# Half-width expert blocks behind the full ones in a two-layer AdaLN kernel with a mixture of experts

## The chip, the cores and the metric

The kernel runs on one core of a Trainium2 chip. The metric is the device time of one execution in microseconds. A profile shows the busy time of five engines: TensorE (PE, with its weight loads as PEld), VectorE (DVE), ScalarE (ACT), GpSimd (POOL) and the queue of SyncE (SP), which issues most DMAs.

## The reference, cut to what matters

Two AdaLN blocks over 8 sequences (b = 0 to 7) of 512 tokens and 128 channels, all float32:

```python
# layer 0
h = layernorm(x) * (1 + ca) + sa
x = x + ga * attention(h)                  # 16 heads of 8 channels, low-rank terms in q, k, v, o
h = layernorm(x) * (1 + cb) + sb
x = x + gb * moe(h)                        # 8 experts, 2 per token, 128 -> 512 -> 128, and a shared expert
# layer 1
h = layernorm(x) * (1 + ca) + sa
x = x + ga * selective_ssm(h)              # convolution, projection, scan along the sequence, projection
h = layernorm(x) * (1 + cb) + sb
x = x + gb * ffn(h)                        # pointwise convolution, 8 experts with gates (all computed), RMS norm, FFN
```

The part that is changed is `moe`: a router picks two of eight experts for each token, each expert is gelu(h W1 + b1) W2 + b2 with a hidden width of 512, the two results are weighted by the router's probabilities, and one shared expert is added for all tokens.

## The kernel before, in words

The program has three stretches. First comes the attention of layer 0, written as a row of "slots"; events that belong to the layer-0 experts (router, ranks, places, scatters) are hung on slots too. Then come "ticks": one pass of the loop at L1771 per block of expert work, with events of layer 0's routing of the last sequence and of layer 1's SSM hung on tick numbers by `when(t, ...)`. Last comes a tail of events without ticks, in which the experts of layer 1 are computed; it begins at tick number n, the number of blocks.

**Routing.** The eight sequences are in two parts, `PB = (6, 2)`: part 0 is b = 0 to 5, part 1 is b = 6 and 7. `place` gives each token a row within its expert's region of a DRAM tensor `x_rows[h]`, and `scatter` (L802) writes tokens there, with indirect DMAs on POOL. When all tokens of a part are placed, `table(h, step)` (L818) works out, on DVE and POOL, how many blocks of 256 rows (BLK) each expert has; the blocks of all experts stand in one row. There are `NBLK[h]` places for them: the number of full blocks that the tokens make, plus 7, because each of eight experts may leave its last block partly empty. That is 31 for part 0 and 15 for part 1. For each block the table holds the expert (`of`), the first row (`row0`) and the biases. `rows_back` (L881) works out where each token's two results will stand in `y_rows`.

**Ticks.** `work` (L1592) is the list of blocks: 31 routed blocks of part 0, 12 blocks of the shared expert for part 0, 15 routed blocks of part 1 and 4 of the shared expert, n = 62 in all. At tick i TensorE transposes the input of block i + 2 (`turn_in`, pxt), runs `up` of block i (L1056: ph, four matmuls of 256 columns, each followed by a gelu on ACT) and `down` of block i - 1 (L1064: pyb, eight matmuls of 128 columns, then a copy on ACT). A float32 matmul shows as two in the profile. For a routed block (`routed`, L949) the SP queue reads `of` and `row0` into registers and issues four DMAs: `xg` (the block's 256 rows, four ticks ahead), `w1b` and `w2b` (the expert's two weight matrices, 256 KB each, three and two ticks ahead, three buffers each) and `y_rows` (the result). A shared block (`everyone`, L1006) has its weights at hand and needs only `hl`, one load for two blocks.

**Behind the routed blocks of part 0.** From tick 32 on (`t0`, L1688) 48 indirect DMAs on POOL (`gather`, L1084) bring each token's two results back, and `combine` (L1098) adds them on DVE, weighted, to the shared expert's result. Then follow, per sequence, the statistics, the modulation and the convolution of the SSM (on DVE and ACT), the projection of four sequences at a time (`ssm_project`, pj), a chain of elementwise steps on ACT, DVE and POOL with a scan (`chain`, L1623), the projection out (`ssm_out`, py) and the lead-in to layer 1's FFN (`lead_in`, L1630): `ffn_pointwise` (L1383, pw), logits, ranks, gates. The gates of the first sequence go out at tick 61. The gathers and SSM of part 1 run in the tail beside layer 1's experts, whose products `t` are formed on DVE, and for odd experts of b = 0 to 3 on POOL (`expert_gate`, L1498).

**Order.** Each engine's instructions stand in the order in which the program pins them. DMAs on SP are placed in that queue by the scheduling layer.

Of the kernel before, what the change touches and what calls it, by code (L numbers as in the profile page):

```python
# [30 lines left out]

BLK = 256
# [3 lines left out]
NBLK = tuple(2 * n * S // BLK + NE - 1 for n in PB)  # L36
# [32 lines left out]
def tile_adaln_two_blocks(  # L69
# [144 lines left out]
    def folded(out, src):  # L214

        lead, n = list(src.shape[1:-1]), src.shape[-1]
        flat_n = math.prod(lead)
        names = "abc"[: len(lead)]
        sizes = dict(zip(names, lead))
        while n > 1:  # L220
            n //= 2
            if n > 1:
                dst = stat.tile([P, NC4 * NE * n], FP, tag=f"fold{n}", name=f"fold{n}", bufs=1)[:, 0 : flat_n * n]
                dst = dst.rearrange(f"p ({' '.join(names)} n) -> p {' '.join(names)} n", n=n, **sizes)
            else:
                dst = out.unsqueeze(len(lead) + 1)
            cut = (slice(None),) * (1 + len(lead))
            G.tensor_tensor(dst, src[cut + (slice(0, n),)], src[cut + (slice(n, 2 * n),)], ALU.add)
            src = dst
# [50 lines left out]
    y_rows = [dram.tile([NBLK[h] * BLK, D], FP, tag=f"y_rows{h}", name=f"y_rows{h}") for h in range(2)]  # L280
# [17 lines left out]
    with tc.tile_pool(name="at", bufs=2) as at, tc.tile_pool(name="sc", bufs=4, space=PSUM) as psc, tc.tile_pool(  # L298
# [371 lines left out]
        for h in range(2):  # L670

            def kept(shape, name, kind=FP):
# [10 lines left out]
                "shift": kept([P, NE], "shift"),  # L683
                "of": kept([P, NBLK[h]], "of", I32),
# [130 lines left out]
        TABLE = 3 + NF  # L815
        blocks = {}

        def table(h, step):  # L818

            hh, n, j = half[h], NBLK[h], CAP[h] // BLK  # L820
# [5 lines left out]
            if step == 0:  # L826
                own = stat.tile([P, NE], FP, tag="own", name="own")
                V.scalar_tensor_tensor(own, count[:, 0:NE], -float(CAP[h]), hh["next"], ALU.mult, ALU.add)
                cmp = tt(NE * j, "cmp").rearrange("p (e j) -> p e j", j=j)
                steps = stat.tile([P, CAP[0] // BLK], FP, tag="steps", name="steps")[:, 0:j]  # L830
                V.tensor_scalar(steps, count[:, 0:j], float(BLK), None, ALU.mult)
# [6 lines left out]
                ends = stat.tile([P, NE], FP, tag="ends", name="ends")  # L838
# [3 lines left out]
                ahead = stat.tile([P, NE], FP, tag="ahead", name="ahead")  # L842
                V.tensor_reduce(ahead, cmp, AX.X, ALU.add)
                V.tensor_tensor(ends, ends, ahead, ALU.add)

                V.tensor_scalar(ahead, ahead, float(BLK), None, ALU.mult)
                V.scalar_tensor_tensor(hh["shift"], count[:, 0:NE], -float(CAP[h]), ahead, ALU.mult, ALU.add)
                blocks["ends"] = ends
            elif step == 1:

                cmb = blocks["cmb"] = tt(n * NE, "cmb").rearrange("p (n e) -> p n e", e=NE)
                V.tensor_tensor(
                    cmb,
                    count[:, 0:n].unsqueeze(2).to_broadcast(shape),
                    blocks.pop("ends").unsqueeze(1).to_broadcast(shape),
                    ALU.is_ge,
                )
                of = tt(n, "of")
# [6 lines left out]
            elif step == 2:  # L865
                wide = tt(n * NE, "wide").rearrange("p (n e) -> p n e", e=NE)
                V.tensor_tensor(wide, blocks["cmb"], hh["shift"].unsqueeze(1).to_broadcast(shape), ALU.mult)
                row0 = tt(n, "of")
                V.tensor_reduce(row0, wide, AX.X, ALU.add)
                V.scalar_tensor_tensor(row0, count[:, 0:n], float(BLK), row0, ALU.mult, ALU.subtract)  # L870
                V.tensor_scalar(row0, row0, float(NE * CAP[h] - BLK), None, ALU.min)
                V.tensor_copy(hh["row0"], row0)
            else:

                f = step - 3
# [5 lines left out]
        def rows_back(h):  # L881
            hh = half[h]
            shape = [P, 2, PC[h], NE]
            tmp = fr.tile([P, 2 * PC[0] * NE], FP, tag="tmph", name="tmph", bufs=1)[:, 0 : 2 * PC[h] * NE]
            tmp = tmp.rearrange("p (k c e) -> p k c e", k=2, e=NE)
            V.tensor_tensor(
                tmp, hh["which"], hh["shift"].unsqueeze(1).unsqueeze(1).to_broadcast(shape), ALU.mult
            )
            yr = stat.tile([P, 2, PC[0]], FP, tag="yr", name="yr", bufs=1)[:, :, 0 : PC[h]]
            V.tensor_reduce(yr, tmp, AX.X, ALU.add)  # L890
# [20 lines left out]
        for i in range(TABLE):  # L911
            at_slot(32 * PB[0] + (45, 47, 49, 59, 60, 62, 63)[i], lambda i=i: table(0, i))
# [34 lines left out]
        shared, turned = {}, {}  # L947

        def routed(h, i):  # L949


            def locate(it):
                it["e"], it["r"] = (
                    nc.values_load(
                        half[h][name][0:1, i : i + 1],
                        engines=[mybir.EngineType.SP],
                        min_val=0,
                        max_val=most,
                        skip_runtime_bounds_check_because="held to the last one by a minimum",
                    )  # L960
                    for name, most in (("of", NE - 1), ("row0", NE * CAP[h] - BLK))
                )

            def fetch(it):
                if "r" not in it:
                    locate(it)
                it["xg"] = fr.tile([P, 2, D], FP, tag="xg", name="xg", bufs=4)
                Q.dma_start(out=it["xg"], in_=x_rows[h][bass.ds(it["r"], BLK), :].rearrange("(c p) d -> p c d", p=P))

            def fetch_1(it):  # L970
                it["w1"] = fr.tile([P, NF * P], FP, tag="w1b", name="w1b", bufs=3)
                Q.dma_start(out=it["w1"], in_=w1t[:, bass.ds(it["e"], 1), :].rearrange("p o f -> p (o f)"))

            def fetch_2(it):
                it["w2"] = fr.tile([P, NF, D], FP, tag="w2b", name="w2b", bufs=3)
                Q.dma_start(
                    out=it["w2"].rearrange("p f d -> p (f d)"),
                    in_=w2t[:, bass.ds(it["e"], 1), :, :].rearrange("p o f d -> p (o f d)"),
                )

            def turn_in(it):
                ps = bank("pxt")
                for c in range(2):
                    pin(T.transpose(ps[:, c, :], it["xg"][:, c, :], ident))  # L984
                it["x"] = fw.tile([P, BLK], FP, tag="xt", name="xt", bufs=3)
                V.tensor_copy(it["x"], flat(ps)[:, 0:BLK])

            def leave(it, py):
                yb = fw.tile([P, 2, D], FP, tag="yb", name="yb", bufs=3)
                A.copy(yb, py[:, 0:2, :])  # L990
                Q.dma_start(
                    out=y_rows[h][BLK * i : BLK * (i + 1), :].rearrange("(c p) d -> p c d", p=P), in_=yb
                )
# [5 lines left out]
                "fetch_2": fetch_2,  # L999
                "turn_in": turn_in,  # L1000
                "first": lambda py: None,
                "leave": leave,
                "bias": lambda f: half[h]["bias"][:, i, f : f + 1],
            }

        def everyone(b, i):  # L1006
# [4 lines left out]
            def fetch(it):  # L1011
# [3 lines left out]
                it["w1"], it["w2"] = ws1, ws2  # L1015
                it["x"] = turned[b][:, BLK * i : BLK * (i + 1)]

            def turn_in(it):
# [4 lines left out]
                it["gt"] = fw.tile([NE + 1, BLK], FP, tag="gt", name="gt", bufs=4)  # L1023
# [15 lines left out]
            def leave(it, py):  # L1039
# [7 lines left out]
                "fetch_2": lambda it: None,  # L1047
                "turn_in": turn_in,
                "leave": leave,
                "bias": lambda f: col("bs1", f),  # L1050
# [5 lines left out]
        def up(it):  # L1056
            ph = pair("ph").rearrange("p a (b t) -> p (a b) t", t=BLK)
            for f in range(NF):
                pin(T.matmul(ph[:, f, :], lhsT=it["w1"][:, f * P : (f + 1) * P], rhs=it["x"], start=True, stop=True))  # L1059
            it["hid"] = fw.tile([P, NF, BLK], FP, tag="hid", name="hid")  # L1060
            for f in range(NF):
                A.activation(it["hid"][:, f, :], ph[:, f, :], AF.Gelu_apprx_tanh, bias=it["bias"](f))

        def down(it):  # L1064
            py = bank("pyb")
            it["first"](py)
            for c in range(2):
                for f in range(NF):
                    pin(
                        T.matmul(  # L1070
                            py[:, c, :],
                            lhsT=it["hid"][:, f, c * P : (c + 1) * P],
                            rhs=it["w2"][:, f, :],
# [790 lines left out]
```

## Time and profile before

| | us |
|---|---|
| median of 6 runs | 1022.19 |
| lowest, highest | 1019.26, 1025.82 |
| the profiled execution | 1020.34 |
| its span, first to last instruction | 1018.5 |

| stretch of the profiled execution | us from the span's start |
|---|---|
| 31 routed ticks of part 0 | 541.8 to 663.8 |
| 12 shared ticks | 663.8 to 720.2 |
| 15 routed ticks of part 1 | 720.2 to 803.5 |
| 4 shared ticks, to the last ph | 803.5 to 830.5 |
| tail | 830.5 to 1018.5 |

The granted clock of TensorE is 0.99 over the span. A row of a group of instructions in the profile reads: line, engine, operation, what it writes <- what it reads, number; busy time and mean duration; idle time of the engine before it and what ended that. Helpers record under one line (L65 for DVE, ACT, POOL and SP), so these are told apart by the names of their tiles.

### The profile page before, as it was taken

What the parts mean: (1) busy time and instruction counts of PE and PEld (TensorE: products, weight loads), DVE (VectorE), ACT (ScalarE), POOL (GpSimd) and SP (SyncE); (2) the same over time, 40 slices, a digit from 0 to 9 for tenths busy, and PEclk for the clock granted to TensorE, in tenths of its full rate; (3) what the DMA queues carried; (4) which work ended last, traced back from release to release, by engine and by line L of the source; (5) the groups of instructions that cost most, each with busy time, mean ns of one, the idle gap of its engine ahead of it and who ended that gap; (6) DMA issues with size and microseconds to landing.
All of it is one profiled execution on the core that took longest, in us unless ns stands there. A gap on an engine that the chain in (4) does not pass through costs nothing.

```text
span 1018.5 us, 24175 instructions
## 1 busy us (share of the span) xinstructions
PE 983.6 (97%) x9540; PEld 649.3 (64%) x9540; DVE 659.1 (65%) x1310; ACT 608.1 (60%) x1335; POOL 479.6 (47%) x755
## 2 busy tenths in 40 slices
PE   9999999999999999999998999999999999898897
PEld 7455455555555545555558999988778666566565
DVE  6777787787877868687723112314787559777863
ACT  1365566666666666666674565545477465585654
POOL 3312133373553736445455213337735257564773
PEclk9999999999999999999999999999999999999899
DMA  6099500000000000000024778652464125223061
GB/s 177 1 287 284 176 3 12 1 12 23 7 28 2 27 8 10 25 2 31 9 80 135 227 241 253 195 147 65 125 167 134 31 66 170 83 81 129 21 214 36
DMA packets 94914, 94.89 MB, mean 93 GB/s; under 512 B 7848, under 2 KB 72832, under 8 KB 94800
## 3 DMA queue, kind: packets, MB, share of 16 engines
q1 hardware_dynamic: 90528, 84.65, 27.4%
q0 software_dynamic: 4096, 8.40, 2.7%
q8 instruction: 75, 1.23, 0.5%
q14 instruction: 39, 0.32, 0.1%
q10 hardware_dynamic: 176, 0.30, 0.1%
HBM read 61.96 MB, written 31.36 MB: 92 GB/s over the span
## 4 chain that ended last, share of the span: by engine, by line
PE 70%; DVE 12%; POOL 9%; ACT 3%; issue 3%; DMA 2%; POOLq 0%; DVEq 0%; SPq 0%; ACTq 0%
PE ps L542 22%; PE av L563 11%; PE pyb L1070 7%; PE ph L1059 7%; PE pm L493 5%; POOL yg L1090 4%; PE pe L1487 2%; PE r L1475 2%; DVE xc L65 2%; PE pqk L451 2%; DVE mpad L65 1%; DVE sh L65 1%; PE pmt L528 1%; PE pw L1387 1%; DVE t L65 1%
## 5 line engine op out<-in xcount | busy, mean ns | idle before, releaser
L65 ACT ACTIVATE es<-ps 128x512 f32<-128x512 f32 x512 | 273.5, 600 | 168.5 <-PE pm L493 125.5
L65 DVE TENSOR_REDUCE mpad<-pm 128x2 f32<-128x1024 f32 (+1 forms) x262 | 308.7, 1194 | 99.0 <-PE pm L493 91.5
L542 PE MATMUL ps<-qt,kt 32*128 32x512 f32 x1024 | 292.4, 629 | 0.5 <-DVE x L65 0.5
L493 PE MATMUL pm<-kt,qt 32*128 32x512 f32 x976 | 260.5, 632 | 0.7 <-DVE mpad L65 0.7
L563 PEld LDWEIGHTS av<-es,vaug 128*32 128x32 f32 x4096 | 104.2, 109 | 94.3 <-ACT es L65 35.9
L542 PEld LDWEIGHTS ps<-qt,kt 32*128 32x128 f32 x1024 | 99.7, 183 | 71.8 <-issue 29.7
L563 PE MATMUL av<-es,vaug 128*32 128x128 f32 x4096 | 137.7, 276 | 0.1
L65 ACT ACTIVATE hid<-ph,bias 128x256 f32<-128x256 f32 x184 | 72.0, 475 | 52.5 <-PE ph L1059 52.3
L807 POOL DMA_INDIRECT x_rows<-tok,ux x64 | 65.4, 1022 | 69.9 <-DMA x_rows<-tok,ux 63.7
L1070 PEld LDWEIGHTS pyb<-w2b,hid 128*128 128x128 f32 x736 | 90.1, 192 | 6.6 <-ACT hid L65 3.8
L1070 PE MATMUL pyb<-w2b,hid 128*128 128x128 f32 x736 | 91.7, 278 | 2.5 <-ACT hid L65 2.5
L1059 PE MATMUL ph<-xt,w1b 128*128 128x256 f32 x368 | 87.9, 382 | 0.0
L493 PEld LDWEIGHTS pm<-kt,qt 32*128 32x128 f32 x976 | 75.3, 183 | 16.6 <-DVE mpad L65 8.2
L1090 POOL DMA_INDIRECT yg<-y_rows,yrows x64 | 64.9, 1014 | 39.1 <-DMA hl<-h_chan 20.7
L65 POOL TENSOR_SCALAR qt<-qf,mask,zero 128x512 f32<-128x512 f32 x31 | 23.8, 767 | 118.2 <-PE pm L493 89.3
L1059 PEld LDWEIGHTS ph<-xt,w1b 128*128 128x128 f32 x368 | 67.0, 192 | 7.4
L1487 PE MATMUL pe<-x,l1w_sb 128*128 128x512 f32 x128 | 65.9, 613 | 1.0 <-ACT ye L65 1.0
L65 DVE COPY xt<-pxt 128x256 f32<-128x256 f32 x46 | 19.1, 418 | 72.2 <-PE pxt L984 72.2
L65 ACT ACTIVATE ye<-pe,pc 128x512 f32<-128x512 f32 x64 | 42.8, 683 | 34.0 <-PE pe L1487 27.0
L1475 PEld LDWEIGHTS r<-l1w_sb,t 128*128 128x128 f32 x368 | 46.9, 194 | 22.1 <-issue 11.7
L1475 PE MATMUL r<-l1w_sb,t 128*128 128x128 f32 x368 | 49.5, 279 | 5.0 <-POOL t L65 2.7
L65 DVE TENSOR_TENSOR t<-ye,gb 128x512 f32<-128x512 f32 x48 | 41.7, 891 | 4.4 <-ACT ye L65 4.0
(304 smaller groups left out, 1481.9 us busy)
## 6 DMA issues: line engine op xcount, KB each, us to landing
x_rows<-zeros SPq DMA_DIRECT2D x16, 1024.0 KB, 10.5
gb<-g_rows SPq DMA_DIRECT2D x32, 512.0 KB, 4.9
w1b<-in_w1t SPq DMA_DIRECT2D x46, 256.0 KB, 3.4
w2b<-in_w2t SPq DMA_DIRECT2D x46, 256.0 KB, 3.4
xg<-x_rows SPq DMA_DIRECT2D x46, 128.0 KB, 3.0
y_rows<-yb SPq DMA_DIRECT2D x46, 128.0 KB, 2.7
x<-in_x SPq DMA_DIRECT2D x8, 256.0 KB, 5.5
h_chan<-hf SPq DMA_DIRECT2D x8, 256.0 KB, 4.3
```

The source lines that it names most:

```text
L65: return lambda *args, **kwargs: self.pin(call(*args, **kwargs))
L451: pin(T.matmul(ps[:, n, :], lhsT=wqk[:, n, :], rhs=d["ht"], start=True, stop=True))
L493: T.matmul(pm[:, i, :], lhsT=qt[r : r + 32, qc * P : (qc + 1) * P], rhs=kt[r : r + 32, :], start=True, stop=True,)
L528: pin(T.transpose(pt[:, c, :], mpads[g // 2 % 2][:, c, :], ident))
L542: T.matmul(ps, lhsT=kt[r : r + 32, kc * P : (kc + 1) * P], rhs=qt[r : r + 32, :], start=True, stop=True)
L563: T.matmul(ps[32 * j : 32 * j + 32, 0, :], lhsT=vaugs[b % 2][:, kc, 4 * j + m, :], rhs=es_of[4 * g + kc, j][:, q], start=(kc == 0), stop=( ...
L807: nc.gpsimd.indirect_dma_start(out=x_rows[h], out_offset=IndirectOffsetOnAxis(ap=chosen["ux", b][:, k, c : c + 1], axis=0), in_=half[h]["t ...
L1059: pin(T.matmul(ph[:, f, :], lhsT=it["w1"][:, f * P : (f + 1) * P], rhs=it["x"], start=True, stop=True))
L1070: T.matmul(py[:, c, :], lhsT=it["hid"][:, f, c * P : (c + 1) * P], rhs=it["w2"][:, f, :], start=(f == 0 and "shared" not in it), stop=(f = ...
L1090: nc.gpsimd.indirect_dma_start(out=gathered[b][:, k, c, :], out_offset=None, in_=y_rows[h], in_offset=IndirectOffsetOnAxis(ap=half[h]["yro ...
L1475: T.matmul(ffn[b]["r"][:, c, :], lhsT=x[:, c * P : (c + 1) * P], rhs=w, start=(start and c == 0), stop=stop, skip_group_check=True,)
L1487: pin(T.matmul(pe, lhsT=l1w_sb[:, 2 + e, :], rhs=x1s[b], start=True, stop=True))
```

## The change

The routed blocks of a part are now of two kinds. Full blocks of 256 rows cover what each expert fills: `FULL` = 17 in part 0 and 1 in part 1, the number that is sure to be filled. What is left of each expert goes into half blocks of 128 rows, `HALVES` = 21 in each part. Two half blocks make one tick, a pair (the last one is single). A pair has the inputs of both halves side by side in one tile, two experts' weights, and therefore two w1b and two w2b loads, two xg loads and two y_rows stores; its `up` runs eight matmuls of 128 columns and eight gelus of 128 columns, its `down` four matmuls for each half. Weight buffers become four of each kind (the fourth in another pool), and the second weights of a pair are fetched one tick later than the first ones (`more_1`, `more_2`).

The order of the ticks is written out as a string: F and D are full blocks and pairs of part 0, f and d those of part 1, S a shared block. In part 1, pairs stand between shared blocks. n becomes 56. The part-0 routed ticks are 28 instead of 31, and all tick numbers of layer 1's events move: the gathers start at 29 instead of 32, and the first gates go out at tick 55 instead of 61, 26 ticks after the gathers' start instead of 29. The table has one more step and a second set of small DVE operations for the half blocks; `rows_back` chooses between two shifts for each token. A row of a block now lies two to a partition (1 KB in one piece) instead of one. Four loads of broadcast rows (`rows_in`) move from ticks 9 to 17 to ticks 26 to 32.

```diff
+HALF = BLK // 2
+FULL = tuple(2 * n * S // BLK - (NE - 1) for n in PB)
+HALVES = 2 * (NE - 1) + NE - 1
+NBLK = tuple(f + HALVES for f in FULL)
...
+        def weights(shape, name):
+            k = n_weights[name] % 4
+            n_weights[name] += 1
+            if k < 3:
+                return fr.tile(shape, FP, tag=name, name=name, bufs=3)
+            return fw.tile(shape, FP, tag=name + "2", name=name, bufs=1)
...
+        def routed(h, some):
+            rows = BLK if some[0] < FULL[h] else HALF
+            parts = [slice(rows * k, rows * k + rows) for k in range(len(some))]
...
+                for k, (_, r) in enumerate(it["at"]):
+                    Q.dma_start(out=it["xg"][:, w * k : w * k + w, :], in_=rows_of(x_rows[h][bass.ds(r, rows), :], k))
+            def fetch_1(it, k=0):
+                for e, _ in it["at"][k : k + 1]:
+                    w1 = weights([P, NF * P], "w1b")
+                    Q.dma_start(out=w1, in_=w1t[:, bass.ds(e, 1), :].rearrange("p o f -> p (o f)"))
+                    it["w1"].append(w1)
...
             for f in range(NF):
-                pin(T.matmul(ph[:, f, :], lhsT=it["w1"][:, f * P : (f + 1) * P], rhs=it["x"], start=True, stop=True))
+                for w1, q in zip(it["w1"], it["parts"]):
+                    pin(T.matmul(ph[:, f, q], lhsT=w1[:, f * P : (f + 1) * P], rhs=it["x"][:, q], start=True, stop=True))
             for f in range(NF):
-                A.activation(it["hid"][:, f, :], ph[:, f, :], AF.Gelu_apprx_tanh, bias=it["bias"](f))
+                for k, q in enumerate(it["parts"]):
+                    A.activation(it["hid"][:, f, q], ph[:, f, q], AF.Gelu_apprx_tanh, bias=it["bias"](f, k))
...
-        work = [routed(0, i) for i in range(NBLK[0])]
-        work += [everyone(b, i) for b in range(PB[0]) for i in range(BLK // P)]
-        work += [routed(1, i) for i in range(NBLK[1])]
-        work += [everyone(b, i) for b in range(PB[0], B) for i in range(BLK // P)]
+        order = "FFFDFDFDFFDFDFDFDFFDFDFDFDFF"
+        N0 = len(order)
+        order += "SSSSSS" + "fSdSdSdSdSdS" + "dSddSdddSS"
...
-        when(9, rows_in, [ga_rows], 4)
-        when(11, rows_in, [gab_rows], 5)
+        when(28, rows_in, [ga_rows], 4)
+        when(30, rows_in, [gab_rows], 5)
-        when(15, rows_in, mpads[0:2], 6)
-        when(17, rows_in, [sb_rows], 7)
+        when(32, rows_in, mpads[0:2], 6)
+        when(26, rows_in, [sb_rows], 7)
...
-        t0 = NBLK[0] + 1
+        t0 = N0 + 1
...
-                (36, 37, 38, 39, 40, 41, 47),
+                (33, 34, 35, 36, 37, 38, 44),
...
-                (50, 51, 52, 53, 54, 57, 58),
+                (46, 47, 48, 49, 50, 51, 52),
...
-        when(44, ssm_project, 0, 0)
-        when(48, ssm_project, 0, 1)
-        when(51, out_weights, 0)
-        chain(0, 49, (0, 0, 1, 1, 2, 2, 3))
+        when(41, ssm_project, 0, 0)
+        when(44, ssm_project, 0, 1)
+        when(47, out_weights, 0)
+        chain(0, 45, (0, 0, 1, 1, 2, 2, 3))
         for b in GROUPS[0]:
-            lead_in(b, 53 + b, (1, 1, 2, 3, 5, 5, 6, 6, 7, 8) if b < 3 else (1, 1, 2, 3, 5, 5, 9, 10, 12, 14))
-        when(59, ssm_project, 1, 0)
+            lead_in(b, 48 + b, (1, 1, 2, 3, 4, 4, 5, 5, 6, 7) if b < 3 else (1, 1, 2, 3, 5, 5, 9, 10, 12, 14))
+        when(53, ssm_project, 1, 0)
...
-            when(n - 3 + k // 3 if k < 8 else n - 5 + k, gather, PB[0] + k // 8, k % 8)
+            when(n - 1 + k // 3 if k < 8 else n - 5 + k, gather, PB[0] + k // 8, k % 8)
...
-            for what, d in ahead:
+            for what, d in (("fetch", 4), ("more_1", 2), ("fetch_1", 3), ("more_2", 1), ("fetch_2", 2)):
                 if i + d < n:
                     work[i + d][what](work[i + d])
```

The numbers in the middle rows of the table of `combine` and SSM times, not shown, move by 3 (b = 1 to 3) and by 3 to 4 (b = 4). `ssm_conv` of b = 5 moves from 57 to 51.

## The prediction

> **What bounds the kernel now.** I read the page's busy times first, then the table of stages, then the chain of what ended last inside single stages, then the DMA issues of the SP queue.
>
> The page's first part and the stage table (columns: stage, its length, then busy time and instruction count of each engine, granted clock, share of the DMA engines, GB/s):
>
> ```profile
> PE 983.6 (97%) x9540; PEld 649.3 (64%) x9540; DVE 659.1 (65%) x1310; ACT 608.1 (60%) x1335; POOL 479.6 (47%) x755
> ```
> ```profile
> 541.80:663.80 122.00, 120.10 (x841) 111.56 (x840) 28.21 (x112) 70.14 (x174) 40.09 (x91) 1.00 0.73 217
> 663.80:750.40 86.60, 84.23 (x544) 70.45 (x542) 44.20 (x124) 44.94 (x113) 57.13 (x67) 1.00 0.41 121
> 750.40:776.70 26.30, 24.53 (x147) 19.93 (x146) 23.06 (x60) 21.17 (x42) 12.10 (x15) 0.94 0.54 149
> 776.70:830.50 53.80, 52.48 (x309) 40.10 (x310) 32.37 (x102) 29.52 (x70) 16.59 (x23) 1.00 0.16 48
> 830.50:862.70 32.20, 30.58 (x180) 21.82 (x180) 24.44 (x46) 19.15 (x33) 25.79 (x25) 1.00 0.53 178
> ```
>
> The first row is the 31 routed ticks of part 0: TensorE is busy all the time and the weight loads for 111.56 of 122.00 us, so nothing but its own work sets the pace. In the second and third rows the weight loads fall to 81% and 76%: TensorE is nearly always "busy", yet it waits for operands. The chain that ended last, taken for 663 to 743 us alone, says for what (first its summary, then pieces, start and length):
>
> ```profile
> by line: POOL yg L1090 47.0%; issue 15.8%; DVE xc L65 10.6%; PE ph L1059 6.5%; DMA hl<-h_chan 5.7%; PE pyb L1070 5.4%; DMA yg<-y_rows,yrows 4.3%; POOL rstd_l1a L65 3.9%; DVE sh L65 1.5%; PE pj L1290 1.3%; ACT hid L65 0.6%; PE pgt L1022 0.5%
> ```
> ```profile
> 663.92 1.73 PE ph L1059 x8
> 665.65 1.78 PE pyb L1070 x16
> 667.65 1.74 PE ph L1059 x8
> 670.04 4.57 DMA hl<-h_chan
> ```
>
> It leaves TensorE at 669.4 us. From 675.1 to 742.8 us it runs through the 48 gathers on POOL, which follow one another every 1.25 us; TensorE fills that stretch but does not set its length.
>
> The SP queue in the first stretch (timeline: start, length, DMA issue), and what it waits for between 547 and 662 us:
>
> ```profile
> 558.82 0.38 SPq L65 DMA_DIRECT2D y_rows<-yb  x1
> 559.72 0.38 SPq L65 DMA_DIRECT2D xg<-x_rows  x1
> 560.67 0.35 SPq L65 DMA_DIRECT2D w1b<-in_w1t  x1
> 562.10 0.34 SPq L65 DMA_DIRECT2D w2b<-in_w2t  x1
> 562.55 0.38 SPq L65 DMA_DIRECT2D y_rows<-yb  x1
> ```
> ```profile
> SPq L65 <- PE pxt L984: 15.8, 16, 1.4
> SPq L65 <- ACT yb L65: 5.8, 3, 4.2
> ```
> Between issues lie two register reads of the tables (median 0.27 us each) and the set-up of the address. All waits of that view add up to 29 us of 115, so SP works 86 us for some 29.5 blocks: **2.9 us per block**, against a tick of 3.73.
>
> **Part by part.** The sum is made on the profiled execution, 1020.34 us (span 1018.5), which is 1.85 below the median of the six runs, 1022.19; I carry the difference over. A measurement here can tell about 0.3%, 3.07 us.
>
> *1. TensorE work of part 0.* A full tick is ph 1.73 + pyb 1.78 + transposes 0.22 = 3.73 us. A pair splits each ph into two matmuls of 128 columns: 16, the number and shape of pyb, so 1.78 instead of 1.73, in all 3.78; the single last half 1.89. Before 31 x 3.73 = 115.6; after 17 x 3.73 + 10 x 3.78 + 1.89 = 103.1. **-12.5.**
>
> *2. SP in part 0.* A pair issues two xg, two w1b, two w2b, two y_rows and reads four table entries: 5.8 us. A full block and a pair take 8.7 us on SP and 7.5 on TensorE. Queue order per tick: y, xg four ahead, the pair's second w1b two ahead, w1b three ahead, w2b. Where ticks alternate, SP falls 1.2 us behind per couple of ticks; over ticks 1 to 22 the queue issues for 31.4 blocks (91.1 us) and six small transfers (2.7), 93.8 us against 85.5 of TensorE work, b=7's steps included: 8.3 us behind. What hides SP's work now, 0.8 us of wait per tick, is used up at the first pair. The second w1b is due two ticks after its issue: 7.5 us, less 3 to 4 of queue ahead of it, less 3.4 of landing, leaves 0.5 us. So all but that shows up as TensorE waiting for a pair's weights: **+8**, bounds 0 (reads cheaper, queue ahead) and 12.5. Data: a block's packets keep 16 engines busy 2.65 us per full tick now; a couple of ticks will need some 7 of 8.7 us, so transfers are not the bound but land later, which is why I don't take less than 8. The Trainium skill, page "DMA: Bandwidth & Descriptors", section "Issuing engines are not separate DMA queues", says that the time a sequencer takes to initiate a DMA is usually small relative to the DMA itself; by that rule this term would be 0 and the forecast 8 us lower, but the rows have SP at work 2.9 us of every 3.73.
>
> *3. Gather stretch.* Its start moves with the end of part 0, if the last y_rows land as soon. In SP's new order the first xg of part 1 and gab_rows (1.95 us to issue at its longest) stand ahead of the last two y_rows, and that xg waits for the last scatter of b=7: issued at 653.4, landed 2.4 us later, 8 us before it is wanted. Later than that, every us would move all 48 gathers. Its length, 675.1 to 742.8, is 48 x 1.25 plus five POOL root steps, all unchanged. TensorE has about 4 us less to do in it (10 ticks less a few pairs), but the second ssm_project, now one tick closer to the convolution before it, waits for that chain instead. **0**, bounds -2 and +3 (pair transfers under the gathers' own, 2.6 us to landing).
>
> *4. From the second pj to the first py*, 26.3 us in row three. One tick fewer (3.73), and chain_4 now shares the tick of the first ssm_out; the chain's own pieces (copies 1.8, table load 1.3, exp and log 1.4, POOL 5.3 from da to ts, scan and product 2.0, others) come to some 17, waits on busy engines to the rest. The convolution of b=4, 3.2 us on DVE, is no longer ahead of the scan: **-3**, bounds -5 and +3.
>
> *5. From the first py to POOL's add of b=3* (823.88). Pairs, b=5's steps and the FFN lead-ins come together in eight ticks that held fewer steps before; counted by the ph and pyb prices TensorE has about 1 us more between these two points; DVE and ACT (a pair's eight gelus: four now take 0.47 each, half-width ones by the copies 0.38 at 256 and 0.27 at 128 some 0.37, so 1.0 us more per pair) are fuller: **+2**, bounds -2 and +6.
>
> *6. Tail.* POOL's order after that add is unchanged but for one rk_eq (0.8) now ahead of it: eight gathers, chain_2, then the first product t:
>
> ```profile
> 823.88 1.12 POOL L65 TENSOR_TENSOR x<-hq,x 128x512 f32<-128x512 f32 x1 [3.48 <-DVE z L65]
> 838.35 1.60 POOL L65 TENSOR_SCALAR da<-dl,asm 32x512 f32<-32x512 f32 x1
> 845.38 1.47 POOL L65 TENSOR_TENSOR t<-ye,gb 128x512 f32<-128x512 f32 x1
> ```
> The sum over experts takes t at 846.9 with no wait now. ffn_pointwise of b=3 moves from the last tick but two to the last but one, so TensorE reaches the sums some 7 us before POOL does. The ticks saved at the end of part 1 (the second half of its own 12.6 us) turn into that wait: **-1**, bounds -1 and +4.
>
> *7. Tables.* table(0) gains 26 small DVE operations of 0.16 to 0.41 us at 506 to 514 us, where DVE idles 1.8 us between others; they hold a PSUM bank of the last scores for up to 3 us: **+1**, bounds 0 and 3. The same in part 1's table and rows_back (8 us of DVE at ticks 21 to 25, DVE 28 of 122 us busy there), the wider bias folds on POOL, the moved row loads and xt's fourth buffer: 0, behind TensorE; without that cover some 3 us.
>
> Sum: -12.5 + 8 + 0 - 3 + 2 - 1 + 1 = **-5.5**: 1014.8 profiled, **1016.7** as a median. Part 1's 12.6 us of TensorE work are not entered beyond terms 4 to 6: they lie beside POOL.
>
> **Rivals.** *Everything counts*: TensorE is the bound to the end and SP keeps up: -25.1, 997. For: 97% on the page. Against: the chain over POOL, and weight loads at 76%. 0.07.
>
> *SP dearer than it looks* (slower): place: part 0, at the pairs' second w1b. Reads of 0.83 and y_rows issues of 1.6 us occur singly now. At 3.4 us per block a couple of ticks costs 10.2; ten couples lose 15 us more: 1020.3 - 5.5 + 15, median 1031.7. It decides from 3.1 us per block, where term 2 reaches 13.5 and the gain is gone. 0.25.
>
> *The second part takes it back*: terms 3 to 6 at +1 to +6 instead of -2, since every engine's queue is in order and three ticks are missing; 1020 to 1025, likeliest 1021.5. For: DVE 23.06 of 26.3 us. 0.23.
>
> *The forecast*, a gain bounded by SP and POOL: 0.45.
>
> The range leaves out the first rival's lower part and the second's upper: 1007 to 1029. Faster by over 0.3%: the forecast except its upper edge, and the first rival, 0.49; within: its edge and most of the third, 0.23; slower 0.28.
>
> **What will show it.** Step 1: 103 us of part-0 work, pair ph near 1.78. Step 2: SP with no wait from the first pair on, and TensorE idle before a ph "<-DMA w1b", 0.5 to 1.2 us per pair; ticks 0 to 27 in 117 us. If these gaps are missing, 8 us too little was forecast. Step 3: first to last gather of part 0 66 to 69 us. Step 4: 23 us. Step 6: a wait of some 7 us before the sums of b=0, on POOL t. Gathers that start later than 11.3 us after the first shared tick's start (675.1 - 663.8 now), or a first product t on POOL later than 181.6 us after it (845.4 - 663.8), would make it wrong upward.

## The result and the profile after

The changed kernel takes 1026.9 us (median of 20 runs, 1023.07 to 1035.1); the kernel before took 1021.36 in the 46 runs beside it. The ratio is 1.0055 (95% interval 1.0041 to 1.007): 5.5 us slower, where 5.5 us less was forecast. The profiled execution has a span of 1026.9 us against 1018.5.

First TensorE's total and the busy times by stage (columns as before; the cuts are first routed ph, first shared tick, second pj, first py, end of the last ph, then the tail):

```profile
PE 970.7 (95%) x9526; PEld 642.2 (63%) x9526; DVE 665.8 (65%) x1360; ACT 606.4 (59%) x1385; POOL 481.4 (47%) x755
```
```profile
548.70:670.00 121.30, 112.24 (x824) 103.64 (x823) 31.53 (x127) 67.43 (x195) 37.56 (x84) 0.99 0.72 221
670.00:753.50 83.50, 79.89 (x564) 69.22 (x563) 46.26 (x141) 47.66 (x133) 60.71 (x75) 1.00 0.56 174
753.50:781.30 27.80, 20.11 (x144) 16.75 (x144) 21.40 (x56) 20.33 (x44) 11.01 (x13) 0.96 0.51 157
781.30:832.10 50.80, 49.32 (x294) 39.34 (x295) 32.89 (x102) 28.12 (x76) 13.38 (x21) 0.92 0.20 59
832.10:865.00 32.90, 24.95 (x132) 17.33 (x132) 19.37 (x36) 16.76 (x29) 25.87 (x25) 0.90 0.42 140
865.00:1026.90 161.90, 144.51 (x810) 97.98 (x808) 112.32 (x236) 95.88 (x224) 94.03 (x88) 0.96 0.29 96
```

TensorE is busy 12.9 us less, though by the prediction's prices some 25 us of its work are gone (12.5 in part 0, 12.6 in part 1): from 100 us on it runs 22.7 us longer at half clock (a granted clock of 0.5 in the profile's records). The span is 8.4 us longer. Row one shows 9 us of idle in part 0, where before had 2, and holds one stretch of 3.4 us at half clock, from 553.6 us. The granted clock, 1.00 in the stages from 776.7 to 862.7 before, is now 0.92 and 0.90. I follow the chain from event to event:

| stretch | before | after | difference | forecast |
|---|---|---|---|---|
| span's start to first routed ph | 541.8 | 548.7 | +6.9 | +1 (term 7) |
| to first shared tick | 122.0 | 121.3 | -0.7 | -4.5 (terms 1, 2) |
| to first py | 112.9 | 111.3 | -1.6 | -3 (terms 3, 4) |
| to POOL's add of b=3 | 47.1 | 51.4 | +4.3 | +2 (term 5) |
| to the end | 194.6 | 194.1 | -0.5 | -1 (term 6) |

The differences add up to 8.4. The profiled execution of after lies 1.85 us above its median and that of before 1.0 below, which leaves the 5.5 of the medians. Of the 6.9, 2.1 are there at the first scores (40 us) already; the same code in the second profile below (`changed_again`) has 0.3 there, so they belong to the run and not to the change.

What TensorE waits for between 548.7 and 670 us (view of waits: us in total, times, longest):

```profile
PE ph L1151 <- DMA w1b<-in_w1t: 3.5, 5, 1.2
PE pxt L1067 <- DMA xg<-x_rows: 2.6, 5, 1.1
PE py L614 <- POOL wo L69: 1.9, 1, 1.9
```

The last line is the only one that this view has for before. Two smaller lines, of pxt waiting for ACT (0.9 us together), are not shown; these waits make up the 9 us of idle.

TensorE's timeline around two places with half clock (start, length, idle before it; ps are the attention's scores, av its weighted values):

```profile
516.44 1.12 PE L546 MATMUL ps<-qt,kt 32*128 32x512 f32 x2 [1.35 <-DVE part L69]
...
537.33 0.66 PE L729 MATMUL ptf<-ident,tok 128*128 128x128 f32 x4 [0.76 <-POOL tok L69]
...
539.96 5.34 PE L567 MATMUL av<-es,vaug 128*32 128x128 f32 x128
```
```profile
781.35 2.04 PE L1458 MATMUL py<-wo,ci 32*128 32x128 f32 x8 [4.84 <-DVE ci L69]
783.32 0.69 PE L1067 MATMUL pxt<-ident,xg 128*128 128x128 f32 x2
783.80 3.62 PE L1151 MATMUL ph<-xt,w1b 128*128 128x128 f32 x16
787.21 2.86 PE L1163 MATMUL pyb<-w2b,hid 128*128 128x128 f32 x16
```

The 128 av matmuls took 3.70 us before; the half clock there lasts 3.4 us from 539.9. The pair's ph behind the 4.84 us wait takes 3.62 us, though 16 such matmuls take 1.95 elsewhere in this trace: the clock is at half for 10.2 us from 778.9.

POOL's add of b=3 and its first product t, which the tail waits for:

```profile
832.77 1.13 POOL L69 TENSOR_TENSOR x<-hq,x 128x512 f32<-128x512 f32 x1 [3.51 <-DVE z L69]
...
854.66 1.32 POOL L69 TENSOR_TENSOR t<-ye,gb 128x512 f32<-128x512 f32 x1
```

They were at 823.88 and 845.38. From t to the end it takes 172.2 us against 173.1: the tail is unchanged and only starts later.

### The profile page after: what moved, and what is told of

Its sections match the earlier page's. It is cut to its first block, busy times and chain, and to the rows that moved or that the text cites. A ratio compares the mean times of both kernels' runs of the same rounds, so it can differ in the third digit from the quotient of the medians.

```text
span 1026.9 us, 24391 instructions
## 1 busy us (share of the span) xinstructions
PE 970.7 (95%) x9526; PEld 642.2 (63%) x9526; DVE 665.8 (65%) x1360; ACT 606.4 (59%) x1385; POOL 481.4 (47%) x755
## 5 line engine op out<-in xcount | busy, mean ns | idle before, releaser
L69 ACT ACTIVATE hid<-ph,bias 128x128 f32<-128x128 f32 (+1 forms) x240 | 74.0, 411 | 58.1 <-PE ph L1151 57.6
L1151 PE MATMUL ph<-xt,w1b 128*128 128x128 f32 (+1 forms) x480 | 79.7, 316 | 3.6 <-DMA w1b<-in_w1t 3.5
L69 POOL TENSOR_SCALAR qt<-qf,mask,zero 128x512 f32<-128x512 f32 x31 | 23.9, 772 | 117.9 <-PE pm L497 89.1
L1163 PE MATMUL pyb<-w2b,hid 128*128 128x128 f32 x624 | 78.0, 278 | 0.5 <-DMA w2b<-in_w2t 0.4
L1163 PEld LDWEIGHTS pyb<-w2b,hid 128*128 128x128 f32 x624 | 76.2, 194 | 2.5 <-DMA w2b<-in_w2t 0.6
L69 DVE COPY xt<-pxt 128x256 f32<-128x256 f32 (+1 forms) x40 | 16.4, 412 | 84.5 <-PE pxt L1067 84.5
```

Of the source, the lines that this page charges most:

```text
L69: return lambda *args, **kwargs: self.pin(call(*args, **kwargs))
L1151: pin(T.matmul(ph[:, f, q], lhsT=w1[:, f * P : (f + 1) * P], rhs=it["x"][:, q], start=True, stop=True))
L1163: T.matmul(py[:, c, :], lhsT=it["hid"][:, f, c * P : (c + 1) * P], rhs=w2[:, f, :], start=(f == 0 and "shared" not in it), stop=(f == NF - 1),
```

## Experiments

In the first two groups of runs every kernel that was traced had a stretch of some 24 us under the gathers of part 0 in which TensorE ran at half clock, with single matmuls up to 2.8 us apart, and the kernel before took 1043.9 us there; so those kernels are compared by ratio and by stages outside that stretch, and the other two groups (before at 1023.32 and 1020.66) also by time.

### One part at a time

`halves_part0_only`, with 15 full blocks and the old order and lags in part 1:

```diff
-FULL = tuple(2 * n * S // BLK - (NE - 1) for n in PB)
+SPLIT = (True, False)
+FULL = tuple(2 * n * S // BLK + (-(NE - 1) if s else NE - 1) for n, s in zip(PB, SPLIT))
...
-        order += "SSSSSS" + "fSdSdSdSdSdS" + "dSddSdddSS"
+        order += "S" * 12 + "f" * 15 + "S" * 4
```

> Halves and pairs in part 0 only; part 1 keeps its 15 full blocks and the order and lags it had before, 3 ticks earlier. Theory A (part 0 gains nothing because the SP queue paces it, and the loss of the change arises in front of part 0 and in part 1): first routed ph to first shared tick 119 to 122 us (122.0 before), the rest from there 354 to 356 us as before, time 1021 to 1025. Rival B (part 0 does gain its forecast 4.5 us and the second part alone takes it back): that stretch at 117 us, time 1016 to 1018.

`halves_part1_only`: `SPLIT = (False, True)`, 31 full blocks first, events of part 1 three ticks later than in the changed kernel.

> Part 0 keeps its 31 full blocks; part 1 has the changed order of half blocks and the shared expert's pieces with the shortened lags, 3 ticks later than in the changed kernel. Theory A (the shortened chain of part 1 costs by itself 2 to 4 us): from the first shared tick to the end 356 to 359 us against 354.7 before, time 1023 to 1026. Rival B (part 1 by itself gains or costs nothing, all of the loss is part 0's and its table's): 1019 to 1022.

Ratios 1.0056 (1.0033 to 1.008) and 1.0087 (1.0059 to 1.0115): each half of the change loses by itself. The stages say where. From the first routed ph to the first shared tick it takes 118.3 us with halves and 123.5 without; the first routed ph comes at 551.8 with part 0's new table and at 543.5 with the old one. TensorE's row for that end of the attention, first the kernel with the new table, then the one with the old:

```profile
512.00:552.00 40.00, 37.38 (x448) 21.88 (x441) 9.98 (x43) 18.62 (x41) 18.87 (x34) 0.79 0.22 66
```
```profile
512.00:543.50 31.50, 29.64 (x463) 18.22 (x452) 7.45 (x30) 18.64 (x42) 18.55 (x34) 1.00 0.29 87
```

The same attention work, at a mean clock of 0.79 and of 1.00. And from the first py to the fourth it takes 18.7 us with part 1 as before and 23.3 with the changed order. Of theory A, the loss in front of part 0 and the cost of part 1's order hold, with larger sizes than it had. That part 0 itself gains nothing does not hold: its 118.3 us lie between theory A's 119 and rival B's 117, and 3.7 us below the kernel before.

### SP or the transfers

`y_stores_on_act`:

```diff
-                    Q.dma_start(out=rows_of(y, k), in_=yb[...])
+                    (A if h == 0 else Q).dma_start(out=rows_of(y, k), in_=yb[...])
```

> The changed kernel, its 38 stores y_rows of part 0 issued from ACT's queue instead of SP's; bytes and order of the loads stay. Theory S (SP's time for issuing is the limit: 3.2 us per block by the trace, 77.6 us of work in 80 us): SP falls to 2.7 us per block, the 12.8 us that TensorE waits for w1b and xg in part 0 fall below 5, first routed ph to first shared tick 112 to 114 us instead of 121.3, time 1018 to 1020. Rival D (the transfers themselves are late, 221 GB/s and 0.72 of the DMA engines, whoever issues): the waits stay above 10 us, time 1025 to 1028.

Part 0's routed ticks (stage table; then all that is left in the view of waits):

```profile
550.90:660.00 109.10, 107.21 (x823) 101.59 (x822) 29.97 (x125) 66.97 (x194) 33.31 (x76) 1.00 0.84 257
```
```profile
PE py L614 <- POOL wo L69: 1.9, 1, 1.9
```

109.1 us instead of 121.3, no wait for w1b or xg at all, while the same bytes run at 257 GB/s instead of 221. So the transfers had room, and SP's queue was the limit; rival D is out. Whether its own work or the waits that a store brings into its order weigh more, this run does not part. The 12 us are not the price of SP alone, since the 121.3 hold 3.4 us at half clock and the 109.1 none. The unedited changed kernel in its second profile has the same stores on SP and the full clock:

```profile
546.80:664.80 118.00, 109.88 (x824) 102.26 (x823) 31.19 (x125) 67.02 (x195) 37.41 (x84) 1.00 0.76 228
```

In the five profiles of this kind (`changed_again`, `halves_part0_only`, `chain_first`, `table_spread`, `busy_before_py`) the stretch takes 117.5 to 118.6 us, so like for like SP cost 8.4 to 9.4. The ratio is 1.0041 (1.0026 to 1.0056), not the 0.997 to 0.999 of theory S: its profiled run had lost 9.1 us ahead of the first routed ph, 6.2 of them from 512 us on, where the new table's steps are. The changed kernel was not timed in this group; in the second one, with the same 24 us, it has 1.0116.

### The order on DVE

`chain_first`: the line `chain(0, 45, ...)` moved ahead of the loop that hangs up `combine`, no other edit.

> The changed kernel; the steps of chain(0) are put ahead of the other steps of the same ticks, so that on DVE dl<-dl,u no longer stands behind combine of b=5, which waits 4.8 us for the shared expert's piece of the same tick (768.7 in the trace, u done at 764.9), and on POOL da and ts stand ahead of an add. Theory C (order on DVE makes the late first py, and TensorE's 4.84 us gap there also brings 10.2 us at half clock): from second pj to first py 20 us instead of 24 to 28, no or one 3.4 us window of half clock behind it, POOL's add of b=3 4 to 8 us sooner, time 1019 to 1023. Rival E (TensorE's and ACT's work in these ticks sets the pace): less than 1.5 us, 1025.5 to 1027.

Ratio 1.0093 (1.0069 to 1.0117). dl did come as soon as u was done (790.27 against 790.24), but from the second pj's end to the first py it took 25.3 us, against 23.9 in every other version with the changed order that has its first ssm_out at the same place with nothing put ahead of it. Theory C falls, and DVE's and POOL's timelines show what changed:

```profile
790.96 1.69 DVE L69 SCALAR_TENSOR_TENSOR sh<-yg,gates,sh 128x128 f32<-128x128 f32 x4
794.02 5.26 DVE L69 SCALAR_TENSOR_TENSOR sh<-yg,gates,sh 128x128 f32<-128x128 f32 x4 [1.38 <-ACT sh L69]
```
```profile
794.89 0.69 POOL L69 TENSOR_SCALAR ts<-ts,small 64x512 f32<-64x512 f32 x1
795.55 1.26 POOL L69 TENSOR_TENSOR x<-x,gab_rows 128x512 f32<-128x512 f32 x1
796.78 1.09 POOL L69 TENSOR_TENSOR rstd_l1a<-var,mhalf 128x4 f32<-128x4 f32 x1
797.87 1.26 POOL L69 TENSOR_TENSOR x<-x,gab_rows 128x512 f32<-128x512 f32 x1
```

Four operations that take 1.39 us in the changed kernel's trace took 5.26: two of them lasted 2.0 us each and ended within 0.2 us of the end of a POOL add. Moving dl forward had put POOL's work beside them. The Trainium skill, page "SBUF — State Buffer", section "Who interferes with whom", says that a DVE instruction with two SBUF inputs and a GpSimd instruction that reads SBUF exclude each other; these rows agree.

### The table, the wait before the first py, and all repairs together

`changed_again` is the changed kernel on the chip of this group.

> The changed kernel once more, unedited, as the measure for the other kernels on the same chip: ratio to the kernel before 1.004 to 1.007 if the chip behaves as the first one did; up to 1.009 if the 24 us stretch at half clock under the gathers, seen in the four kernels above, comes up on this chip too.

Ratio 1.0116 (1.0066 to 1.0166), with the 24 us stretch: above the 1.009 expected, though the interval reaches below it.

`table_spread`:

```diff
-            at_slot(32 * PB[0] + (45, 46, 47, 49, 59, 60, 62, 63)[i], lambda i=i: table(0, i))
+            at_slot(32 * PB[0] + (45, 46, 47, 48, 50, 52, 59, 60, 62, 63)[i], lambda i=i: table(0, i))
...
-        first = [(243 + i, i, "locate") for i in range(4)]
+        first = [(246 + i, i, "locate") for i in range(4)]
```

> The changed kernel with the four DVE steps of table(0) cut into six and issued at slots 45, 46, 47, 48, 50, 52 instead of 45, 46, 47, 49; the first blocks' loads three slots later. Theory T (the extra DVE steps hold back the sums of the last weighed values, so that TensorE waits 1.3 us and loses one to three windows of half clock behind it): the idle before ps '<-DVE part' at 515 us falls below 0.5, no half clock between 510 and 550 us, first routed ph 4 to 7 us sooner than in the changed kernel, time 4 to 6 us below it. Rival P (the later first routed ph is the start of the run, not the table): less than 1.5 us.

Ratio 1.0068 (1.004 to 1.0097), 2.3 us below changed_again in the medians, between theory and rival; the two intervals overlap, so the time alone does not tell them apart. The idle before ps on "DVE part" is 0.19 us instead of the 1.35 shown above, and the time lost to before between 512 us and the first routed ph 2.8 us instead of changed_again's 4.1, but one 3.4 us window at half clock stayed, at 539.1.

`busy_before_py`:

```diff
             wo = held.pop(("wo", b))
+            if b == 0:
+                keep_busy(36)
```

> The changed kernel with 36 idle 128x128 matmuls (some 4 us, into a bank nobody reads) put ahead of the first ssm_out, where TensorE waits 4.8 us for the scan. Nothing else moves, so no work starts sooner by it. Theory K (the waiting itself is free, the 10.2 us at half clock behind it are not): clock 1.0 there, first to fourth py 18.7 to 19.5 us instead of 23.3, POOL's add of b=3 4 to 5 us sooner, time 3.5 to 5 us below the changed kernel. Rival L (the ticks there are paced by ACT and DVE): first to fourth py stays above 22 us, time within 1 us or up to 2 us later.

Ratio 1.0127 (1.0059 to 1.0196): it decides nothing on time. A float32 idle matmul is two instructions; the 72 took 8.70 us, and the first py came 4.4 us later. But behind it the clock was 1.00, so that this stretch shows what the ticks cost without half clock (816.7 to 838.7 us, first to fourth py; before had 18.66 us of TensorE in 18.70):

```profile
816.70:838.70 22.00, 20.51 (x141) 17.00 (x140) 15.83 (x52) 13.11 (x38) 3.41 (x7) 1.00 0.36 108
```

20.5 us of work and 1.5 of waits: 22.0 us where theory K has 18.7 to 19.5, so theory K falls here and rival L's mark is met. Of the 4.6 us that the changed kernel lost between these two points, 3.3 remain at full clock, 1.9 of them more work and 1.4 more waits; its 7.8 us at half clock behind the first py cost 1.3 net, because the slow clock also hides these waits. That is one run; the others with this order, with 4.7 to 7.8 us at half clock there, take 22.9 to 23.3, but for two_repairs_busy below.

`three_repairs`: y_stores_on_act and table_spread, and the first ssm_out with its statistics at tick 49.

> The changed kernel with the y_rows stores of part 0 on ACT's queue, table(0) spread as in table_spread, and the first ssm_out with its two statistics one tick later (49), so that a tick's matmuls fill TensorE's wait. By the sum of the three (12 us in part 0, 5 in front of it, 4.5 after the first py): first routed ph at 543 us, first shared tick 110 us behind it, POOL's first product t 181 us behind that, time 1004 to 1010. Rival G (part 0's gain is taken back before the tail, as the forecast's third rival has it): above 1016.

Ratio 0.9982 (0.9964 to 0.9999), 11 us below changed_again, with the same 24 us stretch in its trace. First routed ph 544.2, the first shared tick 111.3 us behind it. From there to the first py it takes 138.6 us against 138.5 in changed_again, and 23.1 us to the fourth: the moved ssm_out brought nothing. The median lies 2.2 us below before, not the 11 to 17 of the sum, which speaks for rival G: part 0's gain is there at the first shared tick (655.6 us, 664.8 in changed_again) and not at the end. No trace of before with the 24 us stretch shows where it goes.

### Where 1.2% went, without the 24 us

> The kernel before, unedited, for its trace on a chip where it takes 1044 us instead of 1021: the additional 22 us lie in the 48 gathers of part 0 (86 to 93 us from first to last instead of 67.6), with TensorE at half clock and one matmul every 1.7 us, as in the changed kernels here; first routed ph at 541 to 544 us, to the first shared tick 122 us, from the second pj's end to the first py 24 us, first to fourth py 18.7 us. If the 22 us lie elsewhere, the changed kernel has a stall of its own.

`before_here` took 1022.92 us, so the trace that was meant to show the 22 us in the kernel before does not hold them; where that kernel lost them was not seen. Its stages repeat those of the first profile: 541.8, 124.3 (one window at half clock), 111.3 to the first py, 20.4 to the fourth (one window).

`part0_repaired` is halves_part0_only with the two repairs of part 0; `two_repairs` the changed kernel with them.

> Halves in part 0 only, with its y_rows stores on ACT's queue and table(0) spread over six slots; part 1 as before. Theory A (part 0 pays where SP and the table do not take it back; part 1's halves bring nothing, since chain and lead-ins have a length of their own): first routed ph at 542.5 to 545 us, first shared tick 109 to 111 us behind it, 8 to 11 us below the kernel before, ratio 0.989 to 0.993, and below two_repairs by 5 us or more. Rival B (part 1's halves bring some of the gain): within 2 us of two_repairs, or above it.

> The changed kernel with the y_rows stores of part 0 on ACT's queue and table(0) spread, the first ssm_out where the change puts it (tick 48). Against three_repairs (ratio 0.9982) it shows what moving ssm_out one tick is worth: if TensorE's wait for the scan is filled by real work, three_repairs is 2 to 4 us faster, and this has 0.999 to 1.002; if the lead-ins' steps set the pace of these ticks, the two are within 1 us.

part0_repaired: 1016.12 us, ratio 0.9922 (0.9895 to 0.9948). two_repairs: 1017.78, ratio 0.9947 (0.9926 to 0.9968). Both beat the kernel before; the two repairs turn 1.0055 into 0.9947, some 11 us, each ratio from its own group. Of theory A in part0_repaired the stages and the ratio hold (it lies 7.2 us below before), but not the 5 us below two_repairs: the medians are 1.7 us apart, within rival B's 2. Against three_repairs, two_repairs can't be judged by ratio, since the 24 us stretch is in one group only; by stages (22.9 us from the first to the fourth py against 23.1) moving ssm_out is worth nothing. Stages from first routed ph over first shared tick, first and fourth py to the end, first part0_repaired, then two_repairs:

```profile
545.00:656.10 111.10, 109.18 (x824) 102.96 (x823) 27.68 (x106) 66.67 (x194) 33.22 (x77) 0.98 0.82 251
656.10:772.70 116.60, 108.81 (x701) 89.98 (x699) 69.88 (x195) 67.68 (x160) 76.39 (x97) 1.00 0.46 136
772.70:791.40 18.70, 18.70 (x121) 15.72 (x121) 10.64 (x45) 12.42 (x30) 3.28 (x6) 1.00 0.32 98
791.40:1014.30 222.90, 201.39 (x1129) 137.90 (x1128) 153.07 (x326) 129.04 (x293) 129.84 (x126) 0.98 0.28 92
```
```profile
545.20:656.50 111.30, 109.35 (x824) 103.25 (x823) 30.97 (x126) 67.01 (x194) 33.38 (x76) 0.98 0.81 250
656.50:768.10 111.60, 101.58 (x708) 87.34 (x706) 70.08 (x197) 68.45 (x178) 76.06 (x95) 0.98 0.53 160
768.10:791.00 22.90, 22.80 (x139) 19.95 (x139) 15.83 (x52) 13.05 (x38) 4.27 (x9) 0.85 0.34 104
791.00:1013.50 222.50, 195.47 (x1095) 133.75 (x1094) 148.24 (x321) 127.44 (x292) 129.15 (x125) 0.96 0.29 94
```

Rows one and four agree. Row three: part 1's halves cost 4.2 us after the first py. In row two they seem to win 5.0, but 4.6 of these are a wait of part0_repaired's own: its last y_rows store, of 660.4, stood on ACT until 667.0, and the gathers began 15.0 us after the first shared tick instead of 10.4 (ACT's timeline):

```profile
667.00 0.34 ACTq L70 DMA_DIRECT2D y_rows<-yb  x1
667.40 1.57 ACT L70 ACTIVATE hid<-ph,pc 128x256 f32<-128x256 f32 x4 [6.97 <-DMA xg<-x_rows]
```

From the first gather to the first py it takes 101.6 us there, as in before, and 101.2 in two_repairs, so a later first gather moves the first py with it. So part 1's 15 ticks becoming 12 are worth 0.4 us up to the first py, and cost 4.2 behind it. As times the two kernels are not told apart (the intervals overlap); that part 1's halves cost rests on the stages.

`two_repairs_busy`: `keep_busy(14)` at the place of busy_before_py, in two_repairs.

> two_repairs with 14 idle 128x128 matmuls (28 instructions of 0.12 us, 3.4 us) ahead of the first ssm_out, inside the 3.6 us that TensorE waits there; busy_before_py had 72 instructions, 8.7 us, and delayed the first py by 4.4. Theory K (the half clock behind the wait, 3.4 us from 761.2 and 6.8 us from 768.1 in two_repairs, costs 2.4 us after the first py): first py as early as before, first to fourth py 20.5 to 21.5 us instead of 22.9, ratio to the kernel before 0.991 to 0.994 instead of 0.9947. Rival L (the added matmuls and steps of these ticks set the pace): 22.5 us or more, ratio 0.9935 to 0.996.

1014.67 us, ratio 0.9938 (0.9913 to 0.9962), not to be told from two_repairs. The profiled execution is its slowest (1018.79), and shows why filling one wait does not settle it:

```profile
763.81 3.53 PE L428 MATMUL idle<-ident 128*128 128x128 f32 x28
767.72 1.12 PE L1465 MATMUL py<-wo,ci 32*128 32x128 f32 x8 [0.37 <-DVE ci L69]
...
778.91 1.38 PE L1337 MATMUL ptn<-ident,xh 128*128 128x128 f32 x4 [0.72 <-DVE x L69]
780.95 1.65 PE L1465 MATMUL py<-wo,ci 32*128 32x128 f32 x8 [0.66 <-DVE var L69]
782.52 0.47 PE L1072 MATMUL pxt<-ident,xg 128*128 128x128 f32 x1
782.79 3.62 PE L1156 MATMUL ph<-xt,w1b 128*128 128x128 f32 x16
```

The first py is as early as before and the second follows after 5.0 us instead of 8.2. Then TensorE, now quicker, meets two waits of 0.7 us for DVE, and the clock falls to half for 10.2 us behind them. First to fourth py: 26.7 us. By the marks set, rival L holds in this trace and theory K does not; the ratio lies within both. So no run here shows a gain from filling this wait: in this trace the half clock came later instead, and cost more.

## Why the prediction was wrong, term by term

The forecast is missed by 11 us in the medians and by 13.9 in the two profiles. Of the 13.9, 2.1 are the start of the run, 3.8 term 7, 3.8 terms 1 and 2 together, 1.4 terms 3 and 4, 2.3 term 5 and 0.5 term 6. The step that failed in every run with this table is term 7; behind it come terms 4 and 5, and the clock, which no term priced.

**Term 7 (tables, +1, bounds 0 and 3) failed.** Between 512 us and the first routed ph the changed kernel loses 4.8 us to before, and 4.1 to 9.6 in the five other runs with this table in these slots; the old table 0.8. The count and length of the DVE operations were right; that they hold a PSUM bank of the last scores was said and priced as a delay of up to 3 us. The delay at 515 us was 1.9 us, and spreading the table took most of it away. What was missing is the half clock: in four of the six runs 10.2 to 20.5 us of it begin directly behind this wait (20.5 in busy_before_py). In the changed kernel's own profile and in changed_again the clock stays at 1.00 there, and 3.4 us at half clock come some 24 us later, behind a wait of 0.76 us for POOL in the first and behind no wait that the profile shows in the second. table_spread has such a stretch too, at 539.1, so that the table brings it is not shown.

**Term 2 (SP, +8) was right in its cause, as y_stores_on_act shows, and nearly in its size.** Like for like it is 8.4 to 9.4. Terms 1 and 2 together forecast 117.5 us for the stretch, and five profiles have 117.5 to 118.6. Only the changed kernel's own profile has 121.3; about 2 of that are its 3.4 us at half clock (the kernels with the stores on ACT take 110.6 to 111.3 us with such a window in the stretch, and 109.1 without), the rest is open. The account inside the term had gaps. I let 0.5 us remain at each second w1b; xg, issued four ticks ahead, I did not count as late, and it was: 2.6 us of waits against 3.5 for w1b in the view above. The view has 6.1 us for the two together, not the 12.8 that the expectation of y_stores_on_act names. Between 560 and 640 us SP waits 9.4 us in all, less than the 14.6 before, but not none, as I had written. At 2.9 us of own work per block the forecast's price was right; with these waits in queue order it is 3.3 us per block of elapsed time. The rule weighed in the prediction (the Trainium skill, page "DMA: Bandwidth & Descriptors", section "Issuing engines are not separate DMA queues"), that issuing costs little beside the DMA, would have this term at 0; in y_stores_on_act 8.4 to 9.4 us hung on who issues.

**Term 1 (-12.5) was right**: without the waits the stretch is 109.1 to 111.3 us.

**Term 3 (0) was right** within its bounds: gathers 10.2 us after the first shared tick (11.4 before, so 1.2 us are won), 67.6 us from first to last in both.

**Term 4 (-3) was too large.** From the second pj's end to the first py it takes 24.3 us before, 23.9 after, 24.3 with part 1's full blocks: the chain has its own length, and in place of the tick saved TensorE has a wait of 4.84 us. Of the 1.6 us won up to the first py, 0.4 lie here and 1.2 ahead of the gathers.

**Term 5 (+2)** came out at +4.3. In busy_before_py, which has no half clock there, it is +3.0: 1.9 us of it the work that I had counted as 1, the rest waits. So half clock behind the 4.84 us wait makes 1.3 of the 4.3.

**Term 6 (-1) was right** within 0.5 us, and TensorE waits 6.57 us for POOL's t in the sums of b=0, where I had some 7. Product t came 184.7 us after the first shared tick, beyond the 181.6 that I had set as the mark for a forecast too low.

**Not priced at all: the clock.** Between 100 and 840 us TensorE ran 3.4 us at half clock before and 17.1 after. Terms 4, 5 and 7, which put waits in place of TensorE's work or among it, had this cost behind them. The rows of before showed such windows (one at 770.3 us, behind a wait of 1.54); I read the clock column as a property of the chip and not as a cost of waits. The Trainium skill, page "TensorE: Matmul & The Clock Gate", section "Why this matters for your kernels", warns of idle gaps above about 3 us. The traces are stricter: half clock follows waits of 1.34 us (515 us in halves_part0_only) and 1.91 us (550 us in the changed kernel), two of 0.7 within 2.8 us, and one of 1.00 in two_repairs, where the 16 matmuls behind it take 3.58 us:

```profile
760.09 3.58 PE L1168 MATMUL pyb<-ws,hid 128*128 128x128 f32 x16 [1.00 <-ACT hid L69]
```

A wait of 1.90 at 543.7 in the first profile of before brought none, and in the second profile the same wait did. The page's section "What's actually happening" has a free-running window of 3413 ns, and the stretches at half clock here are 3.4 us long or multiples of that. A wait that falls into one such window in one run and across two in the next would fit this; no run here tests it.

So no rival came true as such. The second rival's SP price was not reached: term 2 stays near 9, where that rival has 13.5. Terms 3 to 6 come to +2.2, inside the third rival's +1 to +6, and the 3.0 us that stay at full clock fit its fuller ticks; the half clock beside them it did not name. Term 7's loss in front of part 0 was in no rival. That the two repairs reach a ratio of 0.9947, the forecast's own -5.5 us, is luck: they take term 2 away, which the forecast had at +8.

## What to carry to other kernels

Taking work off a busy TensorE is a gain only where the queue that feeds it keeps the new pace: count SP's elapsed time per block, its waits included, against the shorter tick, and move stores to another queue before cutting the tick. Where a change turns TensorE's work into waits of a microsecond or two, price the half clock that can follow them, with a spread from run to run: at the end of the attention 10.2 to 20.5 us of it followed in four of six runs, and in ticks that wait for other engines anyway 7.8 us of it cost 1.3. Filling the wait with idle matmuls brought no gain that these runs can tell. And a latency chain over four engines does not get shorter because fewer ticks lie beside it.

## What the runs showed of the hardware that was not expected

In the first two groups TensorE, with no wait that the profile shows, issued single matmuls up to 2.8 us apart for some 22 us beside the first gathers (y_stores_on_act):

```profile
685.97 0.37 PE L1163 MATMUL pyb<-ws,hid 128*128 128x128 f32 x1 [0.85 <-issue]
688.07 0.37 PE L1163 MATMUL pyb<-ws,hid 128*128 128x128 f32 x1 [1.73 <-issue]
690.20 0.37 PE L1163 MATMUL pyb<-ws,hid 128*128 128x128 f32 x1 [1.76 <-issue]
```

All eight kernels traced there have it, from 679 to 698 us on; the kernel before ran 22 us longer in both groups. In the third group, on the same chip as the second, it was gone. What brings it stays open.
